# A gated convolution layer: making the gate's blocks as a partner of the first chunk, by seven products of half blocks for eight, and keeping them on chip

## The chip, the core and the metric

The kernel runs on one core of a Trainium2 chip. The core has engines that work side by side, each through its own list of instructions in order: TensorE (PE in the profile, with its weight loads as PEld), VectorE (DVE), ScalarE (ACT), GpSimd (POOL) and SyncE (SP), which here only issues transfers. ACT issues transfers too, from the same list as its arithmetic. Semaphores tie the lists together. TensorE writes into PSUM, eight banks of 128 partitions by 512 numbers; the other engines read it from there. All numbers are float32, and a written matmul of 128x512 appears in the trace as two records.

The metric is the device time of one execution in microseconds (us).

## What is computed

The kernel computes four layers on one image `x` of 512 channels by 64 by 64 pixels, each `x = x + layer(group_norm(x))`: an attention layer, two gated convolution layers (L1 and L2, the same code with other weights) and a linear attention layer. The change is in the gated layers:

```python
fused = conv1x1(x, w_in, b_in)             # 512 -> 1024 channels
pwa = fused[:, :128]                       # the gate
abc = fused[:, 128:]                       # 7 chunks of 128 channels
dw_abc = dwconv7(abc, dw_w, dw_b)          # 7x7, each channel by itself
dw0, dw1, dw2 = dw_abc split into 128, 256, 512 channels
h = pwa * dw0
h = conv1x1(h, pw0_w, pw0_b) * dw1
h = conv1x1(h, pw1_w, pw1_b) * dw2
return conv1x1(h, w_out, b_out)
```

The group norm subtracts a mean for each group of 16 channels and scales by the reciprocal of its standard deviation.

## The kernel before

**Tiles.** `X` holds the image on chip: 128 partitions, 4 chunks of channels (NC), 4096 pixels (N) in 8 blocks of 512 (NB). Each of the 1024 rows of `w_in` belongs to one of 8 chunks of 128: chunk 0 of the array is the gate, 1 to 7 are the inputs of the seven convolutions. In the code before, `w_in[i]` is the weight of convolution `i` (array chunk `1 + i`), and the gate's weight is a tile of its own, `w_gate`.

**Norm.** At the start of a layer `_group_params` makes the means (`less`) and the scale (`gn_r`, line 123). The scale goes into the weights (`centered.scaled`: line 360 on DVE for the first weight, line 357 on ACT, four instructions each, for the others), the mean is subtracted from `X` block by block (`centered.take`, line 349, on ACT, four instructions a block).

**Making the inputs.** A block of one chunk made directly (`product`) takes four matmuls, one for each chunk of `X`. `fused(0, k)` makes convolution 0's input so, blocks 0 to 7. `gate(0, b)` makes the gate's block b so, late: it is multiplied at once into the result of convolution 0, in one DVE instruction that reads PSUM (line 1129). The six other inputs are made in pairs of chunks and pairs of blocks (`group(i, k)`): four blocks, by seven products of two matmuls each in place of eight (`_Seven.steps`, Winograd's form of Strassen's scheme). That needs sums of the two weights (`w_sum`, four DVE instructions a pair, line 400) and differences of X (`diff`, eight DVE instructions a group, line 413; one buffer). Of the seven steps, the first two each leave a result that ACT copies out (`kept`, two buffers, line 1071), the third adds two matmuls to the first's bank and finishes one block, the sixth finishes the second and the seventh the other two. While a group runs, most of the next group's `diff` is made between its steps.

**Planes.** A finished input block goes to one of two on-chip tiles (`plane`; even and odd blocks have one each, so a block waits until the one two before it is out) and by a transfer on ACT's queue (line 851) to `F` in memory. It gets there by ACT (line 861) or by DVE (line 866 or 869). The convolution (`_PlaneConv`) loads `S` from `F` and the taps `T` on SP's queue (`load`, lines 879 and 895); ACT copies half of `S` over (line 902); then 8 parts of 48 small matmuls each run, DVE turns the results (lines 956 and 962), and ACT adds the bias.

**Order.** `convolve(i, first, between)` issues the first loads of convolution i, then the work in `first`, then spreads `between` over the parts, with a weight for each piece. Which piece goes where is written by hand at the end of `_gated_convs` (lines 1193 to 1206). PE keeps the order of the program; on the other engines a scheduler orders the instructions when the kernel is built.

**Buffers.** The pool `cw2` has five tiles of 128 by 512 for `w_in`, `w_sum` and `w_out`; `w_gate` has its own in `cw`. The pool `ch` has five tiles of 128 by 4096, for `diff` and the seven `D[i]`. PSUM has four banks for products and four for convolutions.

## Time and profile before

| | |
|---|---|
| median of 3 runs | 3883.81 us (3882.87 to 3885.79) |
| profiled execution | 3884.6 us, its span 3882.9 us |
| granted TensorE clock, mean | 0.994 |
| layer 1, from its first `gn_ps` to the next layer's | 2276.81 to 2770.83 |
| layer 2, the same | 2770.83 to 3263.35 |
| matmul records `ps<-X,w_gate_L` | 128, 592 ns each, 2376.1 to 2905.5 |
| matmul records `ps<-X,w_in_L` | 320 |
| `diff` instructions in the two layers (line 413) | 192, 682 ns each |

Times in a row are microseconds from the start of the span. A timeline row has its start, its length, the engine, the line, what is written and read, and in square brackets how long the engine had been idle and what released it. A matmul's recorded length overlaps the next one's, so the distance from start to start is the cost in a stream. In a table of groups the last columns are busy time, mean length, and idle time before with its releaser.

### The profile page before, as it was taken

The page shows a single profiled execution, that of the slowest core. Times are in us where ns is not written, and L with a number is a line of the kernel's source. Part 1 is how long each engine was busy: PE and PEld are TensorE (multiplying, and loading weights), DVE is VectorE, ACT ScalarE, POOL GpSimd, SP SyncE. Part 2 cuts the span into 40 slices and gives each one's busy share as a digit, 9 for nine tenths or more (in the row PEclk, how much of TensorE's full clock was granted, in tenths as well). Part 3 has the DMA queues.
Part 4 walks back from the last instruction along what each step waited for, and adds up shares of the span by engine and source line. Part 5 has one row for each costly group of instructions (what it writes and reads, how often), then busy time and mean ns, then how long its engine had stood idle before and what let it go on. Part 6 is the DMA issues. An engine that isn't in the chain of part 4 may idle for free. (4 is left out here: it accounts for less than half of the span.)

```text
span 3882.9 us, 81692 instructions
## 1 busy us (share of the span) xinstructions
PE 3789.8 (98%) x35462; PEld 1682.9 (43%) x35462; DVE 2605.4 (67%) x3106; ACT 2046.6 (53%) x2957; POOL 111.3 (3%) x94
## 2 busy tenths in 40 slices
PE   6999999999999999999999989999999999999999
PEld 4533335333354333453333335454455544455544
DVE  5677774777757777747767755776657667675435
ACT  3677763777736777546655645552255522354210
POOL 0000000000000000000000000000000000121110
PEclk9999999999999999999999999999999999999999
DMA  2000000000000000000000025662156621563334
GB/s 98 9 1 1 1 1 9 1 1 1 1 1 9 1 1 1 1 9 1 1 1 1 1 92 172 180 183 66 40 171 177 186 61 50 153 174 90 94 95 140
DMA packets 194012, 221.56 MB, mean 57 GB/s; under 512 B 13400, under 2 KB 138584, under 8 KB 193520
## 3 DMA queue, kind: packets, MB, share of 16 engines
q1 hardware_dynamic: 166832, 157.12, 14.9%
q10 hardware_dynamic: 26784, 59.11, 4.2%
q8 instruction: 280, 4.59, 0.5%
q14 instruction: 84, 0.69, 0.1%
q0 software_dynamic: 32, 0.06, 0.0%
HBM read 156.46 MB, written 59.77 MB: 56 GB/s over the span
## 5 line engine op out<-in xcount | busy, mean ns | idle before, releaser
L647 ACT ACTIVATE pt<-ps_s,A 128x512 f32<-128x512 f32 x2048 | 1286.2, 687 | 534.9 <-PE ps_s L639 527.3
L730 DVE TENSOR_TENSOR acc<-acc,pt 128x1024 f32<-128x1024 f32 x960 | 1178.0, 1227 | 323.7 <-ACT pt L647 296.7
L657 PE MATMUL av<-pt,V 64*64 64x512 f32 x8192 | 1112.5, 590 | 0.9 <-ACT pt L647 0.9
L639 PE MATMUL ps_s<-O,K 64*64 64x512 f32 x8192 | 1111.6, 589 | 0.0
L657 PEld LDWEIGHTS av<-pt,V 64*64 64x64 f32 x8192 | 339.8, 133 | 557.1 <-issue 525.3
L639 PEld LDWEIGHTS ps_s<-O,K 64*64 64x64 f32 x8192 | 334.3, 133 | 553.8 <-issue 307.1
L902 ACT COPY S<-S 32x1295 f32<-32x1295 f32 (+1 forms) x272 | 341.4, 1256 | 210.7 <-DMA S<-F 123.5
L824 PEld LDWEIGHTS ps_cv<-S,T 64*32 64x32 f32 x13824 | 194.4, 106 | 110.2 <-issue 77.6
L824 PE MATMUL ps_cv<-S,T 64*32 64x128 f32 x13824 | 232.7, 274 | 5.5 <-DVE turned L956 2.2
L824 PE MATMUL ps<-h,w_out_L 128*128 128x512 f32 x512 | 228.7, 599 | 1.5 <-DVE X L1141 1.4
L824 PE MATMUL ps<-diff,w_sum 128*128 128x512 f32 x420 | 197.3, 602 | 0.0
L349 ACT ACTIVATE X<-X,gn_less 128x512 f32<-128x512 f32 x120 | 76.9, 710 | 221.5 <-DVE gn_less L102 210.8
L824 PE MATMUL ps<-X,w_in_L 128*128 128x512 f32 x320 | 152.2, 615 | 13.7 <-ACT kept L1071 6.1
L413 DVE TENSOR_TENSOR diff<-X 128x512 f32<-128x512 f32 x176 | 117.3, 684 | 63.3 <-PE ps L824 40.0
L1129 DVE SCALAR_TENSOR_TENSOR h<-ps,vec,h 128x512 f32<-128x512 f32 x112 | 82.4, 748 | 104.4 <-PE ps L824 103.0
L824 PEld LDWEIGHTS ps<-h,w_out_L 128*128 128x128 f32 x512 | 94.3, 190 | 120.2 <-issue 98.7
L824 PE MATMUL ps<-h,pw_L 128*128 128x512 f32 x320 | 144.2, 600 | 1.3 <-DVE plane L869 1.2
L956 DVE STREAM_TRANSPOSE h<-ps_cv 128x512 f32<-128x512 f32 x112 | 109.2, 1048 | 39.9 <-PE ps_cv L824 39.2
L558 PEld LDWEIGHTS ps_v<-wqkv,X 128*128 128x128 f32 x1024 | 119.5, 193 | 17.9 <-issue 12.5
L413 DVE TENSOR_TENSOR diff<-X,diff 128x512 f32<-128x512 f32 x176 | 117.6, 682 | 7.7 <-PE ps L824 4.3
L824 PE MATMUL vkp<-kT,vT 128*128 128x512 f32 x256 | 117.1, 601 | 4.7 <-DVE vT L1500 4.7
L558 PE MATMUL ps_v<-wqkv,X 128*128 128x128 f32 x1024 | 120.7, 276 | 0.0
(175 smaller groups left out, 3074.7 us busy)
## 6 DMA issues: line engine op xcount, KB each, us to landing
T<-in_L_T_dram SPq DMA_DIRECT2D x112, 384.0 KB, 3.7
F<-plane ACTq DMA_DIRECT2D x112, 324.0 KB, 3.3
S<-F SPq DMA_DIRECT2D x224, 162.0 KB, 4.3
row<-G SPq DMA_DIRECT2D x80, 272.0 KB, 3.7
S<-G SPq DMA_DIRECT2D x96, 153.0 KB, 4.2
G<-plane ACTq DMA_DIRECT2D x48, 289.0 KB, 2.3
T<-in_L_T_dram SPq DMA_DIRECT2D x48, 256.0 KB, 3.8
out_dram<-y SPq DMA_DIRECT2D x32, 256.0 KB, 2.0
```

The source lines that it names most:

```text
L349: self.nc.scalar.activation(xs, xs, AF.Identity, bias=less)
L413: yield eng.tensor_tensor(t[j][c], a(c), b(c), ALU.subtract)
L558: nc.tensor.matmul(ps[:, ts(i, P)], X[:, c, ts(b * QT + i, P)], w[:, 2, c, :], start=(c == 0), stop=(c == NC - 1),)
L639: nc.tensor.matmul(ps[ts(half, D), ts(h, BLK)], K[rows, t * P + half * D : t * P + (half + 1) * D], QO[pair][rows, cols], start=True, stop ...
L647: nc.scalar.activation(pt[:, ts(h, BLK)], ps[:, ts(h, BLK)], AF.Exp, bias=A[:, t, h : h + 1])
L657: nc.tensor.matmul(av[half][rows, :], V[keys, t, rows], pt[keys, ts(h, BLK)], start=(t == 0), stop=(t == NT - 1),)
L730: nc.vector.tensor_add(acc, acc, pt)
L824: self.tc.keep_in_program_order(self.nc.tensor.matmul(*args, **kw))
L902: nc.scalar.copy(second, first)
L956: nc.vector.transpose(out, src)
L1129: nc.vector.scalar_tensor_tensor(d, ps, bias, d, ALU.add, ALU.mult)
```

## The change

The gate's weight becomes `w_in[0]`, the convolutions' weights `w_in[1]` to `w_in[7]`, and the pairs are (gate, 0), (1, 2), (3, 4), (5, 6). The first pair's blocks 0 and 1 are made directly, the other three pairs of blocks by seven products each, one group after the other, ahead of convolution 0. Gate blocks go to a new tile `G`, one more user of the five `ch` tiles, in place of a plane; `gate(0, b)` is then a multiplication on chip without a matmul. The means are subtracted for two blocks at a time in the first step of a group. The `w_gate` tile goes and `cw2` gets a sixth buffer; two weights are loaded at the end of a pair in place of one. The lists of work over the convolutions are written anew. In the built program DVE's list at a layer's start no longer has `diff` instructions ahead of line 360's.

```diff
@@ -979,7 +979,7 @@
     nc = tc.nc
     wp = ctx.enter_context(tc.tile_pool(name="cw", bufs=1))
-    w2p = ctx.enter_context(tc.tile_pool(name="cw2", bufs=5))
+    w2p = ctx.enter_context(tc.tile_pool(name="cw2", bufs=6))
     hp = ctx.enter_context(tc.tile_pool(name="ch", bufs=5))
     keptp = ctx.enter_context(tc.tile_pool(name="ck", bufs=2))
     ps_mm = ctx.enter_context(tc.tile_pool(name="ps_mm", bufs=4, space=PSUM))
@@ -994,9 +994,8 @@
             nc.sync.dma_start(out=t, in_=a[f"{layer}_{name}"][i])
             return t
-        w_in = [weights("w_in", 1 + i) for i in range(4)]
-        w_gate = wp.tile([P, NC, P], FP, tag="w_gate", name=f"w_gate_{layer}")
-        nc.sync.dma_start(out=w_gate, in_=a[f"{layer}_w_in"][0])
+
+        w_in = [weights("w_in", i) for i in range(4)]
         pw0 = wp.tile([P, 256], FP, tag="pw0", name=f"pw0_{layer}")
         nc.sync.dma_start(out=pw0, in_=a[f"{layer}_pw0"])
         pw1 = wp.tile([P, 2, 512], FP, tag="pw1", name=f"pw1_{layer}")
@@ -1008,7 +1007,7 @@
         centered.scaled(w_in[0], rstd, nc.vector)
         centered.began()
-        for w in w_in[1:] + [w_gate]:
+        for w in w_in[1:]:
             centered.scaled(w, rstd, nc.scalar)
         def product(w, hs):
@@ -1023,17 +1022,13 @@
             return product(lambda c: w[:, c, :], [pc.pixels(X[:, c, :], k) for c in range(NC)])
+        def taken(k):
+            for c in range(NC):
+                centered.take(pc.pixels(X[:, c, :], k), c)
+
         def fused(i, k):
-            if i == 0 and k:
-                for c in range(NC):
-                    centered.take(pc.pixels(X[:, c, :], k), c)
-            pc.take(
-                i, k, [taking(w_in[i], k)],
-                lambda dst, src: nc.vector.tensor_scalar(
-                    dst, src, vcol(pre + "b_in", 1 + i), None, ALU.add
-                ),
-            )
+            put(i, k, taking(w_in[i], k), None)
         D = {}
@@ -1043,6 +1038,7 @@
         diff = [
             [diff[:, ts(2 * j + c, BLK)].unsqueeze(1) for c in range(2)] for j in range(4)
         ]
+        G = hp.tile([P, N], FP, tag="h", name="gate")
         b_in = vall(pre + "b_in").rearrange("p (i n) -> p i n", n=2)
         step_b = small.tile([P, 4], FP, tag="step_b", name="step_b")
         nc.vector.tensor_sub(step_b, b_in[:, :, 1], b_in[:, :, 0])
@@ -1050,7 +1046,7 @@
         def more(n):
             while len(w_in) < n:
-                w_in.append(centered.scaled(weights("w_in", 1 + len(w_in)), rstd, nc.scalar))
+                w_in.append(centered.scaled(weights("w_in", len(w_in)), rstd, nc.scalar))
         def summed(i):
             t = [w2p.tile([P, NC, P], FP, tag="w", name="w_sum") for _ in range(2)]
@@ -1067,21 +1063,26 @@
         def keep(i, j, ps):
             t = keptp.tile([P, BLK], FP, tag="kept", name="kept")
-            bias = step_b[:, (i + 1) // 2 : (i + 1) // 2 + 1] if j else vcol(pre + "b_in", 1 + i)
+            bias = step_b[:, i // 2 : i // 2 + 1] if j else vcol(pre + "b_in", i)
             nc.scalar.activation(t, ps, AF.Identity, bias=bias)
             return t
         def put(i, k, ps, more):
-            short = i % 2 == 0 and k % 2 == 0
-            pc.put(
-                i, k, ps, more, vcol(pre + "b_in", 1 + i),
-                step_b[:, i // 2 : i // 2 + 1] if short else None,
-            )
+            bias = vcol(pre + "b_in", i)
+            if i:
+                short = i % 2 and k % 2 == 0
+                pc.put(
+                    i - 1, k, ps, more, bias, step_b[:, i // 2 : i // 2 + 1] if short else None
+                )
+            elif more is None:
+                nc.scalar.activation(G[:, ts(k, BLK)], ps, AF.Identity, bias=bias)
+            else:
+                nc.vector.tensor_add(G[:, ts(k, BLK)], ps, more)
         def bank(j):
             return ps_mm.tile([P, BLK], FP, tag="mm", name="ps7")
-        made = [(i, k) for i in (1, 3, 5) for k in range(NB // 2)]
+        made = [(i, k) for i in (0, 2, 4, 6) for k in range(NB // 2)][1:]
         made = {g: differences(g[1]) for g in made}
         def group(i, k):
@@ -1108,24 +1109,27 @@
                 steps[n]()
                 for _ in range({2: 2, 5: 4}.get(n, 0)):
                     next(after, None)
+                if n == 0 and i == 0:
+                    for b in (2 * k + 2, 2 * k + 3) if k + 1 < NB // 2 else ():
+                        taken(b)
                 if n == 6 and k == NB // 2 - 1:
-                    more(min(i + 4, NDW))
+                    more(min(i + 6, NDW + 1))
             return [(0.5, lambda n=n: step(n)) for n in range(7)]
         def gate(i, b):
             h = [D[c][:, ts(b, BLK)] for c in range(min(i, 3))]
+            d = D[i][:, ts(b, BLK)]
             if i == 0:
-                ps = taking(w_gate, b)
-                bias = vcol(pre + "b_in", 0)
-            elif i < 3:
+                nc.vector.tensor_mul(d, d, G[:, ts(b, BLK)])
+                return
+            if i < 3:
                 ps = product(lambda c: pw0[:, ts(i - 1, P)], h[:1])
                 bias = vcol(pre + "pw0_b", i - 1)
             else:
                 ps = product(lambda c: pw1[:, c, ts(i - 3, P)], h[1:])
                 bias = vcol(pre + "pw1_b", i - 3)
-            d = D[i][:, ts(b, BLK)]
             nc.vector.scalar_tensor_tensor(d, ps, bias, d, ALU.add, ALU.mult)
         def output(chunks, b, o):
@@ -1148,7 +1152,7 @@
         def blocks(f, i):
-            n = (4, 1, 1, 2, 2, 2, 2)[i]
+            n = (0, 1, 1, 2, 2, 2, 2)[i]
             return [(n / 4, lambda b=b: f(i, b)) for b in range(NB)]
         def inputs(i):
@@ -1190,18 +1194,25 @@
             for _, f in between:
                 f()
-        b12, b34, b56 = (inputs(i) for i in (1, 3, 5))
+        b12, b34, b56 = (inputs(i) for i in (2, 4, 6))
         g = [blocks(gate, i) for i in range(NDW)]
-        for b in range(NB):
-            fused(0, b)
-            if b == 2:
-                for _ in made[1, 0]:
-                    pass
+        fused(0, 0)
+        taken(1)
+        fused(1, 0)
+        for b in (2, 3):
+            taken(b)
+        fused(0, 1)
+        for _ in made[0, 1]:
+            pass
+        fused(1, 1)
+        for k in range(1, NB // 2):
+            for _, f in group(0, k):
+                f()
         convolve(0, b12[:10], b12[10:])
-        convolve(1, g[0][:3], g[0][3:] + b34[:12])
-        convolve(2, [], b34[12:])
-        convolve(3, g[1] + b56[:2], g[2] + b56[2:12])
-        convolve(4, [], b56[12:])
+        convolve(1, b34[:6], g[0] + b34[6:20])
+        convolve(2, [], b34[20:] + g[1] + b56[:2])
+        convolve(3, g[2] + b56[2:4], b56[4:16])
+        convolve(4, [], b56[16:])
         convolve(5, g[3], outputs(3))
         convolve(6, [], g[4] + outputs(4))
         for _, f in g[5] + g[6] + outputs(5, 6):
```

## The prediction, made before the changed kernel was run

> **What bounds the kernel now.** First the page's busy line, to see which engine has no slack:

> ```profile
> PE 3789.8 (98%) x35462; PEld 1682.9 (43%) x35462; DVE 2605.4 (67%) x3106; ACT 2046.6 (53%) x2957; POOL 111.3 (3%) x94
> ```

> TensorE (PE) is busy for 98%. An average hides stages, so next the windows of the first gated layer, cut at the start of the layer, the end of its first-chunk products, the start of the gate's products and their end. After the length come the busy times:

> ```profile
> core 0: us, PE busy (x) PEld busy (x) DVE busy (x) ACT busy (x) POOL busy (x), PEclk, DMA share, GB/s
> 2275.00:2314.50 39.50, 31.88 (x73) 14.68 (x74) 16.32 (x37) 25.29 (x48) 3.06 (x3) 0.85 0.41 149
> 2314.50:2376.10 61.60, 60.61 (x877) 30.30 (x876) 40.97 (x66) 32.72 (x35) 0.00 (x0) 1.00 0.59 176
> 2376.10:2413.80 37.70, 37.70 (x641) 19.52 (x639) 16.38 (x27) 23.45 (x22) 0.00 (x0) 1.00 0.61 168
> ```

> In the gate's window PE has no idle time at all; only the layer's start has much. So a product left out shortens the layer, unless PE then waits. What a product costs comes from the gate's own rows in PE's timeline:

> ```profile
> 2376.15 10.46 PE L824 MATMUL ps<-X,w_gate_L 128*128 128x512 f32 x24
> 2386.54 1.59 PE L824 MATMUL ps_cv<-S,T 64*32 64x128 f32 x96
> ```

> 24 records take 10.39 to the next row, 0.09 of it for changing to the convolution's shape, so 0.429 us a record. One written matmul leaves two records. The waits come from the second layer. Its start, VectorE (DVE) and then PE:

> ```profile
> 2774.37 0.17 DVE L122 TENSOR_SCALAR gn_t<-gn_t 128x4 f32<-128x4 f32 x1
> 2774.45 0.69 DVE L413 TENSOR_TENSOR diff<-X 128x512 f32<-128x512 f32 x1
> 2775.05 0.16 DVE L123 TENSOR_TENSOR gn_r<-gn_r,gn_t 128x4 f32<-128x4 f32 x1
> 2775.12 0.69 DVE L413 TENSOR_TENSOR diff<-X 128x512 f32<-128x512 f32 x1
> 2775.72 0.69 DVE L360 TENSOR_TENSOR w_in_L<-w_in_L,gn_r 128x512 f32<-128x512 f32 x1
> ...
> 2776.56 31.97 PE L824 MATMUL ps<-X,w_in_L 128*128 128x512 f32 x68 [3.26 <-DVE w_in_L L360]
> 2808.36 1.88 PE L824 MATMUL ps<-diff,w_sum 128*128 128x512 f32 x4
> ```

> PE waits for the scaled weights (L360), and two `diff` instructions stand ahead of those. And a change from one group of seven products to the next, with no convolution between them:

> ```profile
> 2818.92 1.13 DVE L869 SCALAR_TENSOR_TENSOR plane<-ps,step_b,kept 128x128 f32<-128x128 f32 x4 [0.22 <-PE ps L824]
> 2821.53 0.69 DVE L866 TENSOR_TENSOR plane<-kept 128x512 f32<-128x512 f32 x1 [0.89 <-DMA F<-plane]
> 2822.63 0.69 ACT L1071 ACTIVATE kept<-ps,vec 128x512 f32<-128x512 f32 x1 [1.83 <-PE ps L824]
> 2823.37 1.98 PE L824 MATMUL ps<-X,w_in_L 128*128 128x512 f32 x4 [1.11 <-ACT kept L1071]
> ```

> The old group's last block waits for the one `plane` buffer of its parity to be written out; only then are both `kept` buffers free, the new group's first `kept` follows, and PE's third product waits for it. Over both layers:

> ```profile
> PE ps L824 <- ACT kept L1071: 6.1, 5, 1.9
> ```

> With the 1.2 us in two waits for `plane` (L869) that is 7.3 us, 3.7 a layer.

> **The change, part by part.**

> *Products.* Before, the gate and the first chunk take 8 blocks x 4 matmuls x 2 records each, 128 records a layer. After, the first pair of blocks is still made directly (2 blocks x 2 chunks x 8 records = 32); the other three pairs take 7 products of 4 records, 84. 128 - 116 = 12 records a layer, 24 in all: 24 x 0.429 = **-10.3 us**. The share saved is thus 3 pairs in 4. The changed program keeps 112 changes of matmul shape a layer, so these cost nothing new.

> *The start.* In the changed lists L123 follows L122 and L360 follows L123, with no `diff` between. Small dependent DVE steps stand 0.2 apart (L121 to L122), so L360 starts at 2774.76 in place of 2775.72: 0.96 earlier. In the first layer L122 starts at 2281.09 and L360 at 2282.84; 2281.47 is possible, less about 0.3 that its first DVE instruction spends on waits: 1.1. PE follows. Together **-2.1**; bounds 0 (an X block or weight comes later than L360) and 2.3.
> ScalarE (ACT) gets more to do here: four fills (0.69 each) that DVE did, and two `kept`, among its 28 centering instructions (0.64, four in 2.56). I laid its list against PE's: the first group's first `kept` comes some 0.2 late; taken below.

> At the start PE runs at half rate: 68 records take 30.75 us in the first layer and 31.80 in the second against 68 x 0.429 = 29.2, so 1.6 and 2.6 are lost, in stretches of 3.3 and 5.2 us. I let these losses stay.
> [...]

> *Group changes with the gate.* Three a layer are back to back. The gate's blocks go to chip memory, so only one chunk writes planes, each parity once per group: the last write is 12 us (7 x 1.716) old, against 3.43 from issue to reuse (first layer, 2324.00 to 2327.43). So only L869 counts: above it ends 1.4 after the old group's last product (2818.66), then the DMA's issue takes 0.33 and `kept` 0.69, 2.4 us in all, while PE has two products of the new group, 3.43. **0**, with 1.0 to spare; bounds 0 and 1.9 (the longest such wait).
> At the change to the next pair ACT also scales two newly loaded weights (8 x 0.30); behind them in its list stand the last F0 write and `kept`, and behind their loads in SP's list the loads of convolution 0. The second weight's buffer is free two products before the change (3.4), the load lands in 2.7 (median; 4.6 at most), four scalings take 1.2: done 0.5 after the change, before L869 is (1.4). **0**; with 4.6 it would be 2.4, and `kept` just in time (2.4 + 0.33 + 0.69 = 3.4). Convolution 0, which needs F0, has 20 matmuls (17.2 us) ahead of it still.

> *Where the gate's cover is gone.* Before, 24 gate records bridged the end of convolution 0; they needed nothing that was late. After, the six steps of the next pair stand there (6 x 4 records, as long), but their second product needs `w_sum`, which on DVE stands behind the convolution's four last transposes (4 x 1.21), nine `diff`, `kept` and plane instructions of the old group (9 x 0.605, their spacing), its last fill (1.05) and, itself counted, takes 0.34 more: 11.7 us. PE has five and three-quarter products over it, 9.8. **2.0 a layer** of new wait; bounds 0 and 4. The eight multiplications of g[0] (0.69 from the `diff` row, SBUF alone) replace eight of 0.75 and stand behind that.
> Elsewhere, a layer: the change (2,0) to (2,1) keeps 1.0; two later changes of groups, laid out the same way with the convolutions' transposes in DVE's list, get 0.4 and 1.4; the pw0 block keeps 0.6; the start 0.2. With 2.0 that is 5.6 against 3.7: +1.9 a layer, **+3.8**; bounds 0 and 8.

> Sum: -10.3 - 2.1 + 3.8 = **-8.6**. The profiled execution took 3884.6 (span 3882.9 and 1.7 around it): 3876.0. The runs' median, 3883.81, lies 0.8 lower: **3875.2**. The rest of the kernel, attention and last layer, is untouched.

> **Rivals.**
> 1. *The waits don't grow* (3.7 a layer): -12.4, 3871.4. For it: the longest listed wait, 1.9, stood at a change of groups that now has convolution work in it. Against: the DVE list above.
> 2. *The lost cover costs double*, as the pair's steps depend on DVE and ACT where the gate's did not: 2.0 more a layer, -4.6, 3879.2. For: DVE has 41 of 61.6 us busy in such stretches. Against: six steps follow, so the backlog can drain.
> 3. *The half-rate stretch ends at its own time*, however early PE starts: at half rate a microsecond more holds half a microsecond of work, so 1.05 of the 2.1 is gained, -7.55, 3876.3. For: stretches of 3.3 and 5.2 us don't count from a layer's start. Against: two stretches are few.
> 4. *Slower: ACT's list holds PE at the new back-to-back changes.* Each of three costs the 1.9 seen, the fourth, behind the loaded weights, 1.9 + 2.7: 10.3 a layer, 20.6 - 8.6 = +12.0, 3895.8. It decides from 4.3 a layer on. For: ACT's DMA issues wait for DVE in the same list. Against: planes are 12 us old.

> **How the numbers follow.** Forecast 0.50, rival 1 0.18, rival 2 0.17, rival 3 0.10, rival 4 0.05. 0.2% (7.8 us) is about what a measurement of this kernel tells from no change: faster means under 3876.0. The forecast lies close to that; 0.44 of its 0.50, rival 1 and 0.04 of rival 3 are faster: 0.66. Slower is rival 4, 0.05; the rest, 0.29, is the same. The range 3871.0 to 3880.0 takes in rivals 1 to 3 and leaves out rival 4 and the unlikelier ends of the bounds. The forecast's own is 3873.5 to 3877.

> **What would show it.** After: `w_gate`'s 128 records gone, `ps<-X,w_in_L` 304 in place of 320, the three other product groups 120 more together (24 fewer in all); L360 about 1 us earlier against `gn_ps`; no wait for `kept` at the gate's three changes; one wait of about 2 us for `w_sum` after convolution 0's end. Wrong would be: waits of over 1 us at those changes, or a convolution 0 that starts late because F0's last write stands behind the weights.

## The result, and the profile after

| | before | after |
|---|---|---|
| median (22 runs each) | 3883.51 us (3879.98 to 3888.34) | 3878.95 us (3875.54 to 3881.91) |
| first profiled execution, span | 3882.9 us | 3874.9 us |
| ratio of the times, 95% interval | | 0.9986 (0.9980 to 0.9992) |

The ratio is 5.4 us less, with 3.1 and 7.8 as the ends: a gain, but within the 0.2% that were set as the bound of "no change". The forecast had 8.6 less and 3875.2; the time is 3.75 above that and inside the range. The two profiled executions alone differ by 8.0. That gap between a pair of profiles and the medians is the main question below.

The page's busy line of the changed kernel:

```profile
PE 3780.6 (98%) x35438; PEld 1678.4 (43%) x35438; DVE 2644.7 (68%) x3194; ACT 2063.4 (53%) x2983; POOL 111.4 (3%) x94
```

35462 - 35438: the 24 records are gone. The first gated layer's windows, cut at the start, the end of the directly made pair of blocks, the end of the three groups with the gate, and 64.6 us behind (length, busy times by engine, granted clock, DMA):

```profile
2275.80:2301.20 25.40, 18.92 (x40) 8.88 (x41) 10.60 (x29) 21.89 (x41) 3.06 (x3) 0.76 0.40 144
2301.20:2349.20 48.00, 48.00 (x113) 21.28 (x112) 35.22 (x67) 18.80 (x31) 0.00 (x0) 1.00 0.32 101
2349.20:2413.80 64.60, 63.08 (x989) 31.41 (x995) 49.50 (x83) 38.11 (x43) 0.00 (x0) 1.00 0.60 179
```

In the three new groups PE is never idle. The idle time is at the layer's start and where the convolutions run. The second layer's start, DVE and then PE:

```profile
2769.84 0.17 DVE L122 TENSOR_SCALAR gn_t<-gn_t 128x4 f32<-128x4 f32 x1
2770.05 0.16 DVE L123 TENSOR_TENSOR gn_r<-gn_r,gn_t 128x4 f32<-128x4 f32 x1
2770.25 0.69 DVE L360 TENSOR_TENSOR w_in_L<-w_in_L,gn_r 128x512 f32<-128x512 f32 x1
...
2771.09 18.21 PE L824 MATMUL ps<-X,w_in_L 128*128 128x512 f32 x36 [2.32 <-ACT w_in_L L357]
2789.13 1.88 PE L824 MATMUL ps<-diff,w_sum 128*128 128x512 f32 x4
```

L360 follows L123 at once. This layer's first `gn_ps` stands at 2766.51, so PE starts 4.58 behind it, where it was 5.73 (2776.56 - 2770.83). In the first layer it is 5.76 for 6.93. In this row PE's wait is put down to a weight that ACT scales (L357), no longer to L360.

One of the changes between two groups with the gate:

```profile
2311.81 1.13 DVE L869 SCALAR_TENSOR_TENSOR plane<-ps,step_b,kept 128x128 f32<-128x128 f32 x4 [0.24 <-PE ps L824]
...
2313.25 1.88 PE L824 MATMUL ps<-diff,w_sum 128*128 128x512 f32 x4
2313.45 0.69 ACT L1067 ACTIVATE kept<-ps,vec 128x512 f32<-128x512 f32 x1 [5.37 <-PE ps L824]
...
2314.97 1.88 PE L824 MATMUL ps<-X,w_in_L 128*128 128x512 f32 x4
```

The last plane instruction of the old group ends 0.3 before the first product of the new one has left anything to copy; ACT, idle for 5.37, takes `kept` at once, and PE's products stay 1.72 apart. The end of convolution 0 in the first layer:

```profile
2398.27 1.88 PE L824 MATMUL ps<-X,w_in_L 128*128 128x512 f32 x4
2401.35 1.98 PE L824 MATMUL ps<-diff,w_sum 128*128 128x512 f32 x4 [1.20 <-DVE w_sum L400]
```

That is the new wait, 1.20 and 0.95 in the two layers. The waits of both layers that bear on the forecast (total, times, longest):

```profile
PE ps L824 <- ACT kept L1067: 6.0, 8, 1.3
...
PE ps L824 <- DVE w_sum L400: 2.2, 2, 1.2
...
PE ps L824 <- DVE h L1133: 1.2, 3, 0.4
PE ps_cv L824 <- issue: 1.0, 2, 0.6
```

### The profile page after: what moved, and what is told of

Read it like the earlier page. It is cut to its first block, busy times and chain, and to the rows that moved or that the text cites. A ratio compares the mean times of both kernels' runs of the same rounds, so it can differ in the third digit from the quotient of the medians.

```text
span 3874.9 us, 81766 instructions
## 1 busy us (share of the span) xinstructions
PE 3780.6 (98%) x35438; PEld 1678.4 (43%) x35438; DVE 2644.7 (68%) x3194; ACT 2063.4 (53%) x2983; POOL 111.4 (3%) x94
## 3 DMA queue, kind: packets, MB, share of 16 engines
q8 instruction: 280, 4.59, 0.5%
## 5 line engine op out<-in xcount | busy, mean ns | idle before, releaser
L824 PEld LDWEIGHTS ps_cv<-S,T 64*32 64x32 f32 x13824 | 193.8, 105 | 110.6 <-issue 70.1
L824 PE MATMUL ps_cv<-S,T 64*32 64x128 f32 x13824 | 232.3, 273 | 5.2 <-DVE turned L956 2.2
L824 PE MATMUL ps<-diff,w_sum 128*128 128x512 f32 x492 | 231.6, 602 | 2.2 <-DVE w_sum L400 2.2
L824 PE MATMUL ps<-h,w_out_L 128*128 128x512 f32 x512 | 228.7, 599 | 1.5 <-DVE X L1145 1.4
L413 DVE TENSOR_TENSOR diff<-X 128x512 f32<-128x512 f32 x200 | 133.8, 686 | 83.5 <-PE ps L824 45.7
L824 PE MATMUL ps<-X,w_in_L 128*128 128x512 f32 x304 | 147.7, 618 | 11.5 <-ACT kept L1067 6.0
L824 PEld LDWEIGHTS ps<-h,w_out_L 128*128 128x128 f32 x512 | 94.3, 190 | 120.2 <-issue 98.7
L824 PE MATMUL ps<-h,pw_L 128*128 128x512 f32 x320 | 143.6, 599 | 1.4 <-DVE h L1133 1.2
L413 DVE TENSOR_TENSOR diff<-X,diff 128x512 f32<-128x512 f32 x200 | 134.3, 686 | 11.6 <-PE ps L824 10.5
L824 PEld LDWEIGHTS ps<-diff,w_sum 128*128 128x128 f32 x492 | 90.5, 190 | 110.4 <-issue 99.9
L824 PE MATMUL vkp<-kT,vT 128*128 128x512 f32 x256 | 117.0, 600 | 5.5 <-DVE vT L1511 5.1
```

Source lines behind the costliest of these rows:

```text
L413: yield eng.tensor_tensor(t[j][c], a(c), b(c), ALU.subtract)
L824: self.tc.keep_in_program_order(self.nc.tensor.matmul(*args, **kw))
```

## The experiments

### Both kernels again, unaltered: again, again2, bagain, bagain2

These four have no edit.

> The changed kernel once more, unaltered, with a second profile. Question: the two profiled executions differ by 8.0 us, the medians of 22 runs only by 4.6. If the half-rate stretches at the starts of the gated layers are a matter of the single execution, their loss (2.4 us in layer 1 and about 2.6 in layer 2 of the first profile) should change by 0.5 us or more here, with the span, while the waits for w_sum (1.20 and 0.95) and kept (2.80 and 3.19) repeat within 0.5. If rather the waits differ between executions, these sums change by over 1 us and the starts repeat. If neither changes and the span is within 1 us of 3874.9, the difference lies in the kernel before or outside the layers.

> The changed kernel once more, unaltered, for a third profile. In its first two, the stretches in which PE waits for nothing that the profile shows (issue) took 1.0 and 3.0 us over the two gated layers, and these layers together 977.3 and 980.0. Theory (these gaps are instructions of PE that arrive late, and vary from one execution to the next): layers of 976 to 977 us plus whatever the gaps add here, each gap ending 1.0 to 1.6 us after a packet of the instruction queue has landed. Rival: the gaps are no cause, and the layers differ by over 1 us at the same gaps.

> The kernel before once more, unaltered, with a second profile. If its first profile (span 3882.9) happened to be a slow one of its kind, this span is 1 us or more shorter and the difference shows in the gated layers (494.02 and 492.52 us between their starts) or outside them. If the layers repeat within 0.5 us, the forecast's base stands and the run-to-run difference lies elsewhere.

> The kernel before once more, unaltered, for a third profile. Its gaps of issue were 1.2 and 0.9 us in the gated layers, and these took 986.5 and 986.4. If the change made such gaps larger by the way it spreads the groups over the convolutions, they stay at about 1 us here, and below those of the changed kernel's repeat; if they only vary, 0.5 to 3 us.

Times: the changed kernel 3879.39 (0.9986, 0.9977 to 0.9995) and 3880.91 (0.9988, 0.9979 to 0.9997) against the kernel before on the same chips; the kernel before against itself 1.0003 (0.9994 to 1.0012) and 0.9991 (0.9982 to 1.0000). So eleven runs can put equal code 3.5 us off. Three comparisons of the change agree on 4.7 to 5.4 less, but the third leans on the 27 runs beside it: against bagain2's eleven runs on the same chip, again2 is 1.7 less in the mean and 0.8 more in the median.

The profiles, in us. "Layers" is from the first `gn_ps` of the first gated layer to that of the layer behind the second; "rest" is the span without it, whose code is the same in both. "Named waits" are those for `kept`, `plane`, `w_sum` and `h`; "half rate" is what the first 68 or 36 products of each layer take over 0.429 each.

| | span | layers | rest | named waits | issue | half rate |
|---|---|---|---|---|---|---|
| before | 3882.9 | 986.5 | 2896.4 | 7.3 | 1.2 | 4.2 |
| bagain | 3880.6 | 986.4 | 2894.2 | 7.7 | 0.9 | 4.2 |
| bagain2 | 3887.3 | 989.6 | 2897.7 | 7.3 | 0.4 | 6.3 |
| after | 3874.9 | 977.3 | 2897.6 | 9.4 | 1.0 | 5.0 |
| again | 3877.6 | 980.0 | 2897.6 | 9.7 | 3.0 | 5.1 |
| again2 | 3879.7 | 980.7 | 2899.1 | 10.8 | 2.6 | 4.0 |
| mean after - mean before | -6.2 | **-8.2** | +2.0 | +2.5 | +1.4 | -0.2 |

The layers gave about what was forecast for them: 8.2 against 8.6, with a standard error of 1.5 as the six values scatter. Two things vary inside them from one execution to the next, the half rate and the gaps of issue. In the first pair of profiles they happened to differ little. bagain's layers repeated within 0.2, and the 2.3 by which its span was shorter lay outside them. again kept its starts and its named waits within 0.3; its layers are 2.7 longer, 2.0 of it gaps, a case that its expectation had not listed. That of again2 was wrong in part: not the gaps alone, the named waits too were 1.4 above the first profile's. That of bagain2 was met on the gaps (0.4), but its layers were 3.1 longer than before's: 2.1 of it is half rate at the starts. A further 1.7 is a second stretch at half rate in its first layer that no column holds. From 2436 to 2442 the granted clock is 0.72, so some 3.4 us ran at half rate, right behind a wait of 1.9 for `kept`; from that wait's end to the next convolution part PE took 7.04, where before took 5.35 behind the same wait. In bagain2 the wait lay within one step of the clock's (2433.30 to 2436.72, PE busy for 44%; such steps are the subject further down), in before it fell across two (85% and 60%).

### What a gap of issue is

The longest is in the kernel called both (further down). PE's rows, then the queues in the 5.3 us ahead of the gap and in the 2.6 us of the gap (packets, MB, share of the 16 engines; packets are counted by their start):

```profile
2507.00 1.56 PE L826 MATMUL ps_cv<-S,T 64*32 64x128 f32 x93
2511.09 0.41 PE L826 MATMUL ps_cv<-S,T 64*32 64x128 f32 x3 [2.53 <-issue]
```

```profile
q1 hardware_dynamic: 750, 0.90, 60.1%
q10 hardware_dynamic: 287, 0.66, 32.7%
```

```profile
q1 hardware_dynamic: 570, 0.47, 81.0%
q10 hardware_dynamic: 84, 0.21, 25.7%
q8 instruction: 1, 0.02, 2.5%
```

PE stops three small matmuls short of a part's 96. From 2503.2 to 2508.5 no packet of the instruction queue starts, while the queues of SP and ACT fill the engines; one starts at 2508.52 and has landed at 2509.55, and PE goes on at 2511.09, 1.54 later. All 44 such gaps in the gated layers of the fourteen profiles end so, 1.27 to 1.72 us behind the landing of such a packet. So PE, as these landings show it, ran out of instructions. The page of the changed kernel has 280 of these packets with 4.59 MB, 16.4 KB each, for twice 35438 instructions, so one brings some 250 (an estimate from these counts). In the dense stretches PE does some 500 matmuls in 20 us (577 from 2540 to 2560 in the changed kernel), each with its weight load: by these counts a packet lasts some five microseconds there, and four start in those 20 us.

With the kernel before and its variants the gaps took 0.4 to 1.5 us in five profiles, with the changed kernel and its variants 1.0 to 4.9 in nine. That the new lists, which set more parts of a convolution close together, cause the rise fits this, but was not tried by itself.

### More traffic: traffic

```diff
             else:
                 nc.scalar.copy(second, first)
+        if self.idle is not None:
+            nc.sync.dma_start(out=self.idle, in_=wT[i, r // nl][:, 0:704])
         return w, S
```

> The changed kernel with one more transfer of 352 KB, which nobody reads, behind each loading of 384 KB of taps and two times 162 KB of planes in the gated layers' convolutions. Theory (PE's gaps of issue are instructions that come late because their packets share the DMA engines with the planes' and taps'): the gaps, 1.0 and 3.0 us in two profiles, grow to 6 us or more, and more of them appear in the dense stretches. Rival (the gaps have another cause): they stay at 1 to 4 us, and what the time grows by is waits for the planes (S, turned) alone.

It took 3911.84 (1.0074, 1.0060 to 1.0087), and its waits were:

```profile
PE ps L825 <- ACT kept L1070: 19.8, 11, 7.6
PE ps_cv L825 <- issue: 3.6, 4, 1.9
```

With 0.3 more on `ps` the gaps are 3.9, inside what the rival said. The test did not separate the two, though: the added transfers hold back the planes' writes (4.1 us to landing in the median of the two layers, 3.5 in the changed kernel), `kept` costs 13 us more, and a PE that waits uses up its instructions more slowly. Half rate came with these waits: the granted clock falls to 0.86, 0.66, 0.79 and 0.79 in windows of 12, 20, 8 and 8 us of the first layer, 24 us at half rate in all, where again has none between the layers' starts. That data packets make the instruction packets late is thus argued from the shares above and not shown.

### The products alone: direct

```diff
-        made = [(i, k) for i in (0, 2, 4, 6) for k in range(NB // 2)][1:]
+        made = [(i, k) for i in (2, 4, 6) for k in range(NB // 2)]
...
-        fused(0, 1)
-        for _ in made[0, 1]:
-            pass
-        fused(1, 1)
-        for k in range(1, NB // 2):
-            for _, f in group(0, k):
-                f()
+        for b in range(NB):
+            fused(0, b)
+            if b + 1 < NB:
+                taken(b + 1)
+            fused(1, b)
+            if b == 2:
+                for _ in made[2, 0]:
+                    pass
+        more(6)
```

> The changed kernel with the first chunk's and the gate's blocks all made directly, with eight products each, and the gate still kept on chip: the saving of products alone is undone. Theory (the products give the time): 24 products of 8 records a pair of chunks in place of 84 + 32, so 12 records a layer more, 24 in all at 0.429 us: +10.3 us against the changed kernel, and the first layer's windows longer by 5.1. Rival (the seven products' waits give back what they save): the w_sum and kept waits at the gate's and convolution 0's end go as well, 2 a layer or more, and it comes out at +6 or less.

3890.68, 11.3 over the changed kernel on the same chip (1.0019, 1.0010 to 1.0028, against its 0.9986: 12.8). The layers are 992.9, 12.9 over again's. The theory holds, though the edit also gives other orders to the groups and the planes' writes, so its waits differ too. Its size is understood: 10.3 for the products, 3.8 more in named waits (13.5 against 9.7), 0.3 less in gaps, 0.7 less at half rate, together 13.1. The rival is out: the wait for `kept` grew.

```profile
PE ps L824 <- ACT kept L1067: 10.4, 8, 1.9
```

### The start alone: start and late

start is the kernel before with the first pair's groups in another order; late is the changed kernel with three unused differences ahead of the reciprocal.

```diff
-        made = [(i, k) for i in (1, 3, 5) for k in range(NB // 2)]
+        turn = {1: (1, 2, 3, 0)}
+        made = [(i, k) for i in (1, 3, 5) for k in turn.get(i, range(NB // 2))]
...
-            if b == 2:
-                for _ in made[1, 0]:
+            if b == 4:
+                for _ in made[1, 1]:
```

```diff
+        diff = hp.tile([P, N], FP, tag="h", name="diff")
+        for c in range(3):
+            x = [pc.pixels(X[:, (c + n) % 2, :], 0) for n in range(2)]
+            nc.vector.tensor_tensor(diff[:, ts(c, BLK)].unsqueeze(1), x[0], x[1], ALU.subtract)
         centered.scaled(w_in[0], rstd, nc.vector)
```

> The kernel before with the groups of the first pair taken in the order 1, 2, 3, 0, so that no difference stands ahead of the first scaled weight: the start's term alone. Theory: PE starts 0.96 and 1.1 us earlier in the two gated layers and keeps it: -2.1 us. Rival (the half-rate stretch ends at its own time): PE starts as early, but the stretch behind is longer by as much, at half rate, so half is kept: -1.0. That nothing is kept: 0, with the loss in the stretch larger by 1 us a layer.

> The changed kernel with three differences that nobody uses ahead of the first reciprocal on VectorE, so that the first product of each gated layer starts about 1.1 us later, where it was before the change. Nothing else is altered. If an earlier start is worth its whole length: +2.2 us in the two layers. If the half rate ends at a step of the clock's own, whenever PE starts: its end stands at the same time after the layer's start as before, the loss at half rate becomes about 0.55 smaller a layer, and the layers get longer by 1.1 together (up to 2.2 where a step is passed).

PE's start moved as meant: in start to 5.75 and 4.57 behind `gn_ps`, in late back to 6.96 and 5.74. The times: start 0.9999 (0.9990 to 1.0008), so 0.4 less with 3.9 less and 3.1 more as the ends; late 0.9993 (0.9984 to 1.0002), again2 beside it 0.9988. Both are too wide for a term of 2.1. The layers of start are 985.0, 2.5 below the mean of before's three; those of late 981.9, 2.6 above the mean of the changed kernel's three (979.3). These totals alone would support a gain of the whole length, but they hold other terms too, and equal code differs by 3 us. The terms say less: of the 2.4 us by which PE starts earlier in start the half rate takes 0.5 back (5.4 against a mean of 4.9), and of the 2.3 later in late it gives 1.2 back (3.5 against 4.7). That is between half and the whole, and two single profiles say no more.

What the half rate did shows in windows at the start of the first layer (length, PE busy, granted clock, DMA), of before, bagain2 and start:

```profile
2272.00:2275.00 3.00, 0.00 (x0) 0.68 0.06 14
2275.00:2284.00 9.00, 1.38 (x5) 0.50 0.76 251
...
2286.00:2288.00 2.00, 2.00 (x5) 0.81 0.61 243
```

```profile
2272.00:2275.00 3.00, 0.00 (x0) 0.65 0.06 14
2275.00:2284.00 9.00, 1.29 (x5) 0.50 0.78 258
...
2288.00:2290.00 2.00, 2.00 (x4) 0.51 0.00 0
```

```profile
2275.00:2284.00 9.00, 1.12 (x4) 0.57 0.56 174
...
2288.00:2290.00 2.00, 2.00 (x4) 0.53 0.64 255
```

In windows of 0.25 us the granted clock of before and of the changed kernel is 1.00 or 0.50, but for those in which it changes. A share of 0.68 over 3.00 is thus 1.92 us at half rate, so in before it runs from 2273.1, and by the 0.81 to 2286.8: 13.7 us. In bagain2 it is 2272.9 to 2290.0, 17.1; in start 2276.3 to 2289.9, 13.6; in the changed kernel (0.90 and 0.99 there) 2274.4 to 2288.0, 13.6; in late 2273.0 to 2286.6, 13.6. Four times a length and once the same and a quarter more: a step of 3.4 us. The windows of 0.25 us give 13.65 and, in the second layer, 10.25 in before, 13.64 and 6.82 in the changed kernel: four and three, four and two times 3.41. In the second layer the clock from 2763 to 2791 is 0.82 in before, bagain and bagain2, so 10.1 us at half rate, and 0.88 in the changed kernel's three, start and late, so 6.7: three steps and two. Its place shifts between executions, and PE's start alone doesn't set its length, since late starts as before does. In the first layer the code of before lost 1.55 to 3.1 us by it. In start the stretch ended 3.1 later than in before and the layer had begun 1.8 later (`gn_ps` at 2278.58 and 2276.81), so it lost 2.85 for 1.58 and gave its 1.18 away; late lost 1.56 where the changed kernel lost 2.39 to 2.50.

What ends the half rate can be read from the same traces, by cutting windows at the steps of 3.41 us. In all 28 stretches, two in each of the fourteen profiles, it ends with the first step in which PE is busy for at least 83% (again2, 2773.78 to 2777.19: 2.84 us busy), and no step with up to 82% ended it (bagain2, 2778.05 to 2781.46: 2.78 us busy). So an earlier start of PE gains only half its length as long as the end stays at the same step, and more than its length where the end moves to the step before. Where the steps lie against the layer's start differs from one execution to the next (in the second layer one ends 4.03 behind `gn_ps` in before and 5.10 in bagain2); over many executions the loss should then not depend on when PE starts, which is argued from these 28 ends and not measured. From their start on, the products ran 2.8 us (again2, 2774.35 to 2777.19) to 6.2 us (bagain2, 2778.68 to 2784.87) at half rate.

### The waits: planes, bplanes, psum, both

planes gives each odd column parity a second plane; bplanes is the same in the kernel before; psum has GpSimd make the sums of the later pairs; both is planes and psum together.

```diff
-                t = sp.tile([P, self.pair, f.fh, f.fw], FP, tag=f"o{oy}{ox}", name="plane")
-                nc.gpsimd.memset(t, 0.0)
-                self.out[oy, ox] = t
+                self.out[oy, ox] = []
+                for n in range(1 if shared or ox == 0 else 2):
+                    t = sp.tile([P, self.pair, f.fh, f.fw], FP, tag=f"o{oy}{ox}{n}", name="plane")
+                    nc.gpsimd.memset(t, 0.0)
+                    self.out[oy, ox].append(t)
...
-        t = self.out[oy, ox]
+        t = self.out[oy, ox].pop(0)
+        self.out[oy, ox].append(t)
```

```diff
-            for _ in seven.sums(nc.vector, w_in[i], w_in[i + 1], t):
+            for _ in seven.sums(nc.gpsimd if i else nc.vector, w_in[i], w_in[i + 1], t):
```

> The changed kernel with a second buffer for the planes of odd column parity. Theory: the waits for kept (8 waits, 6.0 us in both gated layers) come from the one such plane that has to be written out before its next group, so they go but for about 0.5 us each where the fill itself is late: -3 to -5 us. Rival: ACT's or DVE's list is late by itself at these changes, whatever buffer is free, and the waits stay at 5 to 6 us: 0 us.

> The kernel before with the second odd plane. Theory (its waits at the back-to-back changes, 6.1 us for kept and 1.2 for the plane, come from the single plane): 4 to 7 us less than before, which is as much as the whole change under study gave. Rival: the same lists hold at these changes by themselves: 0 to -2 us.

> The changed kernel with the four sums of weights of the second, third and fourth pair made by GpSimd in place of VectorE. Theory: the new wait for w_sum at the end of convolution 0 (1.20 and 0.95 us) comes from VectorE's list, 11.7 us long there, so it goes, while the change by itself shortens VectorE's list by 1.4 us at each pair: -1.0 to -2.2 us. [...]

> The changed kernel with the second odd plane and the sums on GpSimd together. Theory: the two waits have causes of their own, so the gains add up: -4 to -7 us against the changed kernel. Rival: one backlog of VectorE stands behind both, and what one frees the other had freed already: no more than the better of the two alone.

| | median, us | ratio to before, 95% | layers, us | named waits | issue |
|---|---|---|---|---|---|
| planes | 3875.57 | 0.9982 (0.9973 to 0.9991) | 975.4 | 4.8 | 3.5 |
| bplanes | 3877.03 | 0.9978 (0.9969 to 0.9988) | 981.8 | 3.1 | 1.5 |
| psum | 3878.12 | 0.9983 (0.9974 to 0.9992) | 980.0 | 7.7 | 3.9 |
| both | 3873.55 | 0.9971 (0.9961 to 0.9980) | 974.9 | 3.2 | 4.9 |

Two waits of planes, and two of bplanes:

```profile
PE ps L826 <- DVE w_sum L400: 3.1, 2, 1.5
...
PE ps L826 <- ACT kept L1070: 0.9, 2, 0.6
```

```profile
PE ps L826 <- ACT kept L1074: 1.9, 3, 1.5
...
PE ps L826 <- DVE plane L872: 1.2, 2, 0.6
```

The one odd plane was the cause of the waits for `kept`: they fall from 6.0 to 0.9. Of the 5.1, 0.9 comes back as a longer wait for `w_sum`. The layers are 4.6 shorter than again's. The time is 3.8 less by the medians, as expected, but only 1.6 by the ratios (0.9982 against 0.9986), whose intervals overlap, so the gain in time is not shown by these runs alone.

bplanes takes 8.5 from the kernel before (the interval is 4.7 to 12.0), above its expectation. Its layers are 5.7 shorter than the mean of before's three, and 4.3 of that are named waits. The two waits for the plane itself (1.2), which its expectation counted in, stayed. In time it does at least as well as the change under study, with no change to the products; in the layers the change gave more, 8.2.

psum takes the wait for `w_sum` away entirely, so VectorE's list was its cause, but `kept` is 6.8 and the gaps 3.9, and its time can't be told from the changed kernel's. both comes to 11.3 less than before, by the ratios some 5.9 more than the change alone, as expected; the upper end of its interval (0.9980) is the lower end of the changed kernel's. Against psum beside it, it is 4.6 less, and its layers are 5.1 shorter, so the plane is worth as much with the sums on GpSimd as without; what the sums add is too small to tell. It also has the largest gaps of issue of all. That PE waits more for instructions where it waits less for data would fit it, but psum, with 7.7 of named waits, has gaps of 3.9, and equal code gave 1.0 to 3.0, so it is not shown.

## Why the prediction was right or wrong

*Right in direction and range, too large by about 3 us.* Step by step:

- *Products, -10.3.* Right: 24 records fewer, `ps<-X,w_in_L` at 304, and direct gives it back.
- *Start, -2.1.* PE's start is 2.3 earlier over the two layers; L360 stands 3.74 behind the second layer's `gn_ps`, where 3.93 was forecast. That the half-rate losses stay was wrong for a single execution: they vary by 2 us between executions of the same code. Means of three came out equal (4.9 and 4.7), so the term is not refuted. Rival 3's mechanism, a half rate that ends by its own time, is what the windows show to within a step of 3.41 us. Its price, half of the term, holds only where the end stays at the same step; over many executions the step rule speaks for the forecast's "let these losses stay".
- *Three back-to-back changes, 0.* Right: no wait for `kept` there in either layer, and 0.22 at the change to the next pair. Rival 4 is out.
- *Lost cover, 2.0 a layer.* The wait stands at the place and on the instruction named, with about half the size: 1.20 and 0.95, in the repeats 2.4 for both. Rival 2 (4.0) is out.
- *All waits, +3.8.* The named waits grew by 2.5. Those for `kept` (3.0 a layer) and `h` (0.6) add up in the first profile to what was forecast for them; the wait for `w_sum` is the term that was sized too large. Rival 1 (0) is out.
- *What was not in the sum.* Gaps of issue, +1.4: "Elsewhere, a layer" counted waits for engines only, and the 1.2 us gap of before's own profile was not used. And +2.0 outside the layers, against "The rest of the kernel, attention and last layer, is untouched": its code is, and its time should be. The other profiles bear that out: the five of before, its repeats, start and bplanes have a mean of 2896.5 there, the eight of the changed kernel and its variants without added traffic 2895.7, each between 2893.3 and 2899.1. So the +2.0 of the six doesn't come back with more profiles, and nothing shows it to be an effect of the change.

So three places kept the sum from the time. Inside the layers the wait for `w_sum` came out at half its size, which made the sum too small a gain, and the gaps of issue were not in it. Products, start and named waits add up to -10.3 - 2.3 + 2.5 = -10.1. Gaps and half rate make it -8.9, and -9.5 if the second stretch in bagain2 is counted; -8.2 was found, and the 0.7 to 1.3 between is not accounted for. The last place is the way from the layers, -8.2, to the -5.4 timed. With the rest of the kernel equal, the 2.8 between them has no term of its own: the layers are known to 1.5 (one standard error) and the time to 2.4 either way, so the two may agree, and whether anything holds them apart stays open. That -8.2 lies so near the forecast's -8.6 is thus partly luck: the wait that was sized too large and the gaps that were left out offset each other. The chance of 0.66 for more than 0.2% rested on a forecast that lay 0.8 us from that bound; with the sizes seen here, it was too high.

## What to carry to other kernels

When the expected gain is a few tenths of a per cent, profile each kernel more than once before a sum is made: two profiles of the same code differed by 6.7 us here, more than the gain. Look for the single buffer behind a repeated wait before saving arithmetic: a second odd plane gave the kernel before 8.5 us of time and 5.7 in the layers, where 24 products and their rescheduling gave 5.4 and 8.2. And where an engine's clock goes by steps, read how a wait lies against them, as the same wait of 1.9 us cost 1.7 more in one of three executions. When a stream of small matmuls is packed more densely, read the instruction queue beside the data queues, since an engine that waits for nothing may be out of instructions, as PE was in the 44 gaps here if their ends are read right.
